# Nested Strassen products for theta and phi, and an earlier data sum in the last image, in an attention and non-local kernel

## The chip, the cores and the metric

The kernel runs on one core of a Trainium2 chip. The metric is the device time of one execution in microseconds. Times within an execution come from the trace of one profiled execution, counted from the start of its span.

## The reference, cut to what matters

The batch is 8 images of 512 channels and 32 x 32 = 1024 positions, all in float32. Everything on TensorE is a 1x1 convolution, which is a matrix product over the channels, or an attention product.

```python
def conv(x, W, b): return einsum('bchw,oc->bohw', x, W) + b
# layer 0: attention with 8 heads of 64 channels
q, k, v = conv(x, Wq, bq), conv(x, Wk, bk), conv(x, Wv, bv)
o = softmax(q^T k / 8) v                      # per image and head
x = x + conv(o, Wp, bp)
# layer 1: non-local block with 256 inner channels, n = 1024
g, theta, phi = conv(x, g_w, g_b), conv(x, theta_w, theta_b), conv(x, phi_w, phi_b)
f = einsum('bcn,bdn->bcd', theta, phi) / n
y = einsum('bcd,bdn->bcn', f, g)
z = conv(y, W_w, W_b) + x
out = (z - mean) * rsqrt(var + 1e-5) * gamma + beta   # mean and var over all images, per channel
```

## The kernel before, in words

**Work of one image.** The loop `for b in range(B)` in the main part goes over the images. For each it does attention (scores `ps`, line 578, and weighted values `po`, line 604), then q, v and k of the *next* image, then the projection `project` (the product of Wp with o, PSUM tiles `pp`), then theta and phi together (`theta_phi`, PSUM tiles `ptp`, result `tp`), then `nonlocal_` (g in `pg`, f in `pf`, `pwf`, and z in `pz`). The last image, number 7, has its own branch: the non-local work of image 6 is done inside it, and the normalization of o comes after that.

**Products.** A convolution is one round of the Strassen-Winograd scheme: the weights are cut in 2 x 2 blocks, the data in 2 x 2 quarters named 11, 12, 21, 22, and seven products replace eight. The table `SEVEN` gives for each product its name, the weight block (0 to 6), the data it takes, its PSUM slot and the parts of the result it is read into. Blocks 3 to 6 are sums of weights; t1 to t4 are sums of data, made by `more_sums` (line 252): t1 = 12 - 11, t2 = 22 - t1, t3 = 22 - 12, t4 = 21 - t2. `seven` (line 342 issues the matmuls) goes through such a table; `between` maps a product's number to work that is emitted after it. `EARLY` and `LATER` are other orders of the seven; the last image's projection uses `LATER`: 11, s1t1, 12, s2t2 and so on. When a product is done, VectorE reads its PSUM slot: `first` (line 766 for theta and phi, with the bias added; line 737 for the projection) or an addition (line 772, line 448).

**Nesting.** For the projection of images 1 to 6 two of the seven products are themselves cut into seven inner products. The table is then `FIVE`, and `nested` (line 299 issues it) yields one inner product at a time; `STEPS` says after which of the 40 matmuls of `FIVE` an inner step is emitted. Inner sums of data come from `inner_parts` (line 264), inner sums of weights lie beside their block in the weight tile (`extra`). Each inner step's PSUM part is read by VectorE at once; two slots alternate, so a step waits until the step two before it has been read. The products of v use inner products whose output has positions on the partitions (`pv_in`, line 418, tiles of 128 columns).

**Theta and phi.** `theta_phi` computes both in one product with positions on the partitions: the plain `SEVEN`, eight matmuls of 128 x 128 by 256 columns each, each matmul two records in the profile.

**Weights.** The weights of one convolution are loaded in units (`UNITS`) into a pool of four buffers of 1792 columns, `wr`, in the order of a plan. Block 0 of some is loaded by itself as "first". `load_w` (its DMA is line 163) issues the next unit on the queue of SyncE (SP). `kept` holds copies in DRAM, with the sums. Theta and phi have two units of 768 KB, blocks (3, 4, 2) and (6, 5, 1). SP issues its DMAs in program order, and a DMA waits for the one eight before it.

**The last image.** After g of image 6, `normalize` multiplies o by the reciprocals of the softmax denominators, in four VectorE operations (line 684) that wait for the tile r (DMAs of line 679); then come t1 and t2 of o. On SP's queue stand, in this order: r (4 DMAs), the first unit of theta and phi, `put_away` (4 writes of g and wf of image 6, lines 906 and 907), `reload` of the z of images 0 to 3 (16 DMAs of 512 KB, line 918), the bias `tpb` (line 752), the second unit of theta and phi, the weights of g, four chunks of z of image 5 (line 925).

```python
            for one in normalize(nxt["d"]):
                one()
            load_w()
            put_away(b - 1)
            for i, tag in enumerate("vqk"):
                reload(i, mats, tag)
            reload(3, foldp, "fold")
        tpb = load_tpb(b)
```

**Image 0.** Its weights are made from the raw ones: sums of blocks on VectorE, then copies to DRAM with `keep`. Its product is plain.

Of the kernel before, what the change touches and what calls it, by code (L numbers as in the profile page):

```python
# [11 lines left out]
ALU = mybir.AluOpType  # L12
# [4 lines left out]
P = 128  # L17
# [13 lines left out]
def unshifted(ctx: ExitStack, tc: tile.TileContext, a: dict, out: bass.AP):  # L31
    nc = tc.nc
# [29 lines left out]
    def pe(ins):  # L62
        tc.keep_in_program_order(ins)
# [47 lines left out]
    for b in range(1, B):  # L111
# [2 lines left out]
    loaded, ahead = [], {"unit": [], "first": []}  # L114

    PAIRS = ((1, 6), (3, 4), (5, 2))
    UNITS = {"WqT": PAIRS, "WkT": PAIRS, "WvT": PAIRS, "WpT": ((1, 2), (3, 4, 5), (6,)), "tp": ((3, 4, 2), (6, 5, 1)),
             "WgT": (range(7),)}
    WIDTH = 14 * P
    INNER = (1, 2)  # L120

    class Weights:

# [4 lines left out]
        def __getitem__(self, at):  # L128
            if not isinstance(at, tuple):
                return self.at[at]  # L130
            return self.at[at[1]][(slice(None), *at[2:])]

        def place(self, n, t):
            size, to = 2 * self.half, 0
            blocks = (0,) if n == "first" else UNITS[self.name][n]
            for i in blocks:
                self.at[i] = t[:, to:to + size].rearrange("p (k f) -> p k f", k=2)
                to += size
                if n != "first" and len(blocks) == 2:
                    self.extra[i] = t[:, to:to + 3 * P].rearrange("p (i f) -> p i f", i=3)  # L140
                    to += 3 * P
            self.tiles[n] = t[:, :to]
            return blocks

        def whole(self, n):
            t = self.tiles[n]
            if n == "first" or len(UNITS[self.name][n]) != 2:
                return t
            return t.rearrange("p (b f) -> p b f", b=2)[:, :, :2 * self.half]

# [52 lines left out]
    def inner_weights(w, i):  # L203

        a11, a12, a22, a21, s2, s3, s4 = w.inner(i)
        return [lambda to=to, l=l, r=r, op=op: dve(nc.vector.tensor_tensor(to, l, r, op))
                for to, l, r, op in ((s3, a11, a21, ALU.subtract), (a21, a21, a22, ALU.add), (s2, a21, a11, ALU.subtract),
                                     (s4, a12, s2, ALU.subtract))]

    def keep_inner(w):  # L210

# [72 lines left out]

    STEPS = [0] * 4 + [1] * 14

    def nested(name, w, data, tags, first, add):

        slots = [bank(tag, f"{name}_in_{tag}") for tag in tags]
        goes_to = {1: ("11", "21", False), 2: ("21", "t4", True)}
        for n, (q, di, begins) in enumerate(goes_to[i] for i in INNER):
            a, d = w.inner(INNER[n]), data[f"inner {di}"]
            pair = slots[::-1] if n % 2 else slots
            begun = set()
            for _, wi, di, s, reads in SEVEN:
                ps = pair[s % 2 if s < 2 else 1][:, s // 2, n % 2 * 256:(n % 2 + 1) * 256]
                pe(nc.tensor.matmul(ps, a[wi], d[di], start=s not in begun, stop=True, skip_group_check=True))  # L299
                begun.add(s)  # L300
                for to, is_first in reads:
                    c = rows(q).start + int(to[0]) - 1
                    at = cols(q).start + (int(to[1]) - 1) * 256
                    (first if is_first and begins else add)((slice(c, c + 1), slice(at, at + 256)), ps)
                yield

    def seven(name, w, data, positions_out, first, add, between=None, early=False,
              by_chunk=False, inner=False):

        nk, half = w.shape[2], w.shape[3]
        tags = list(free)
        free[:] = [tags[3], tags[1], tags[0], tags[2]] if early else [tags[3], tags[1], tags[2], tags[0]]
        slots, begun = {}, set()
        steps, counts = iter(()), iter(STEPS if inner else ())
        if inner:
            free[:] = [tags[1], tags[2], tags[3], tags[0]]
            steps = nested(name, w, data, tags[2:], first, add)

        def read(reads, ps):
            for to, is_first in reads:
                (first if is_first else add)(to, ps)

        products = FIVE if inner else LATER if early == "later" else EARLY if early else SEVEN
        for n, (what, wi, di, s, reads) in enumerate(products):
            if s not in slots or early and what == "t4":
                slots[s] = bank(tags[s], f"{name}_{s}_{n}")
                begun -= {one for one in begun if one[0] == s}
            ps, d = slots[s], data[di]  # L330
            if positions_out:
                parts = [(ps.rearrange("p h (i f) -> p (h i) f", f=half)[:, i, :], i * half // 512,
                          lambda k, i=i: d[:, k, i * P:(i + 1) * P], lambda k: w[:, wi, k, :])
                         for i in range(512 // P)]
            else:
                parts = [(ps[:, m, :], m, lambda k, m=m: w[:, wi, k, m * P:(m + 1) * P], lambda k: d[:, k, :])
                         for m in range(half // P)]
            work = [(*part, k) for part in parts for k in range(nk)]
            if by_chunk and what in ("11", "s1t1"):
                work.sort(key=lambda one: one[4])  # L340
            for i, (to_ps, at, lhsT, rhs, k) in enumerate(work):
                pe(nc.tensor.matmul(to_ps, lhsT(k), rhs(k), start=(s, at) not in begun, stop=(k == nk - 1),  # L342
                                    skip_group_check=True))
                begun.add((s, at))
                for _ in range(next(counts, 0)):
                    next(steps)
            read(reads, ps)
            if between and n in between:
                between[n]()
# [377 lines left out]
            return o["o"], lambda ps: denominators(1, ps), lambda d: normalize((first_den, d))  # L727
        return o["o"], all_denominators, normalize

    def project(b, xt, o, w, between, data=None):  # L730
        def first(q, ps):
            if isinstance(q[0], slice):
                ps = ps.unsqueeze(1)
# [4 lines left out]
                if b == B - 1 and q in ("11", "22"):  # L738
                    dve(ins)

        if not data:
            data = data_sums(quarters_of(o), f"o_{b}", (1, 2), pin=dve)
            between = {**between, 1: lambda: more_sums(data, (3, 4), dve)}
        seven(f"pp_{b}", w, data, False, first, add_to(xt), between, early=b == B - 1 and "later", inner=0 < b < B - 1)


    tps = []
# [7 lines left out]
    def theta_phi(b, w, data, tpb, between):  # L755
        tp = mats.tile([P, NB, 2 * CI], F32, tag="o", name=f"tp_{b}")
        tps[:] = [tp]

        def at(q):
            return tp[:, (int(q[1]) - 1) * NB // 2:int(q[1]) * NB // 2, (int(q[0]) - 1) * CI:int(q[0]) * CI]  # L760

        def as_tp(ps):
            return ps.rearrange("p h (i f) -> p (h i) f", f=CI)

        def first(q, ps):
            ins = nc.vector.tensor_tensor(at(q), as_tp(ps), tpb[:, int(q[0]) - 1].to_broadcast([P, NB // 2, CI]),
                                          ALU.add)
            if q == "11":
                dve(ins)

        seven(f"ptp_{b}", w, data, True, first,
              lambda q, ps: nc.vector.tensor_tensor(at(q), at(q), as_tp(ps), ALU.add),  # L772
              {0: lambda: "t3" in data or more_sums(data, (3, 4), pin=dve), **between})
        return tp

    def f_sums(b, tp, k0):
# [233 lines left out]
    for b in range(B):  # L1010
        last = b == B - 1
        nxt = {}
        if not last:
            nxt["x"] = load_x(b + 1)

# [58 lines left out]
        else:  # L1074
# [1 line left out]
                      {4: lambda: nxt.update(d=denominators(next_bank(f"den_{b}_1")[:, 0, :]))})  # L1076
            z[b - 1] = [held["x"][:, cc, :] for cc in range(CC)]
            between = {4: late_unit(b - 1, 0, sums_now=False)}
            for one in normalize(nxt["d"]):
                one()  # L1080
            load_w()
            put_away(b - 1)
            for i, tag in enumerate("vqk"):
                reload(i, mats, tag)
            reload(3, foldp, "fold")
        tpb = load_tpb(b)
        w = weights("WpT", sums_done=True)
        project(b, xt, o, w, between, nxt.get("o"))
        if b == 0:
            w_p = w  # L1090
        load_w("first")
# [8 lines left out]
            z[b] = [xt[:, cc, :] for cc in range(CC)]  # L1100
        of_theta = []
        w = weights("tp")
        between = {} if last else {5: lambda: b < B - 2 and of_theta.append(f_sums(b, tps[0], 0))}
        if b == 0:
            weight_sums(w, corner["tp"], (3, 4, 5), dve)

            def nest_p(i):
                for one in inner_weights(w_p, i):
                    one()

            between.update({1: lambda: weight_sums(w, corner["tp"], (6,), dve), 2: lambda: nest_p(1), 3: lambda: nest_p(2)})
        tp = theta_phi(b, w, data, tpb, between)
        if b == 0:
            keep("tp", w)
            kept["WpT"] = dict(kept["plain"])
            keep("WpT", w_p, (0,))
            load_w()
        load_w("first")
        load_w(times=2)

        def before_wf():
            if last:
# [243 lines left out]
```

## Time and profile before

| what | value |
|---|---|
| time, median of 3 runs (lowest, highest) | 2118.22 us (2117.09, 2118.61) |
| time of the profiled execution | 2118.56 us |
| its span | 2116.7 us |
| granted TensorE clock, mean over the span | 0.994 |
| TensorE busy | 2090.3 us, 99% of the span |
| VectorE busy | 1403.2 us, 66% |
| ScalarE busy | 790.3 us, 37% |
| GpSimd busy | 525.9 us, 25% |
| moved by DMA | 243.56 MB, 115 GB/s in the mean |

The profiled execution's time is its span and 1.9 us around it; it lies 0.34 us above the median. The page gives averages over the whole span. What a change in one stage is worth has to be read from the timeline, the waits and the chain of work inside that stage.

### The profile page before, as it was taken

The page shows a single profiled execution, that of the slowest core. Times are in us where ns is not written, and L with a number is a line of the kernel's source. Part 1 is how long each engine was busy: PE and PEld are TensorE (multiplying, and loading weights), DVE is VectorE, ACT ScalarE, POOL GpSimd, SP SyncE. Part 2 cuts the span into 40 slices and gives each one's busy share as a digit, 9 for nine tenths or more (in the row PEclk, how much of TensorE's full clock was granted, in tenths as well). Part 3 has the DMA queues.
Part 4 walks back from the last instruction along what each step waited for, and adds up shares of the span by engine and source line. Part 5 has one row for each costly group of instructions (what it writes and reads, how often), then busy time and mean ns, then how long its engine had stood idle before and what let it go on. Part 6 is the DMA issues. An engine that isn't in the chain of part 4 may idle for free.

```text
span 2116.7 us, 33247 instructions
## 1 busy us (share of the span) xinstructions
PE 2090.3 (99%) x13486; PEld 1172.5 (55%) x13486; DVE 1403.2 (66%) x2051; ACT 790.3 (37%) x1045; POOL 525.9 (25%) x392
## 2 busy tenths in 40 slices
PE   9999999999999999999999999999999999999996
PEld 4535863357733677337763377633875348733362
DVE  5587567765578655786557766677565775567636
ACT  1464204642046410564106631166303653066016
POOL 0012900138001370014601155011640119011000
PEclk9999999999999999999999999999999999999998
DMA  6253533244232532425314253133544235222758
GB/s 229 83 148 76 174 147 111 40 92 141 100 117 40 120 110 98 120 40 141 122 62 125 40 152 121 72 101 41 170 139 140 39 63 169 75 31 40 268 188 319
DMA packets 71728, 243.56 MB, mean 115 GB/s; under 512 B 12688, under 2 KB 21136, under 8 KB 69520
## 3 DMA queue, kind: packets, MB, share of 16 engines
q1 hardware_dynamic: 60640, 215.01, 30.4%
q0 software_dynamic: 9072, 24.78, 9.5%
q8 instruction: 108, 1.77, 0.3%
q10 hardware_dynamic: 1856, 1.56, 0.3%
q14 instruction: 52, 0.43, 0.1%
HBM read 160.45 MB, written 47.32 MB: 98 GB/s over the span
## 4 chain that ended last, share of the span: by engine, by line
PE 97%; DVE 1%; ACT 1%; DMA 1%; issue 0%; SPq 0%; DVEq 0%
PE ps L578 21%; PE po L604 21%; PE ptp L342 9%; PE pp L342 7%; PE pv_in L418 6%; PE pq_in L421 6%; PE pk_in L421 6%; PE pg L342 4%; PE pz L342 3%; PE pf L801 2%; PE pp_in_s L299 2%; PE pq L388 1%; PE pq L342 1%; PE pv L385 1%; PE pv L342 1%; PE pk L388 1%
## 5 line engine op out<-in xcount | busy, mean ns | idle before, releaser
L581 ACT ACTIVATE e<-ps 128x1024 f32<-128x1024 f32 x512 | 523.0, 1025 | 422.9 <-PE ps L578 412.2
L587 DVE TENSOR_TENSOR acc<-acc,e 128x1024 f32<-128x1024 f32 x384 | 469.9, 1224 | 103.1 <-ACT e L581 92.9
L578 PE MATMUL ps<-q,k 64*64 64x512 f32 x4096 | 529.3, 589 | 0.0
L604 PE MATMUL po<-e,v 64*64 64x512 f32 x4096 | 528.6, 589 | 0.0
L617 POOL DMA_DIRECT2D fold<-acc x189 | 144.8, 766 | 1358.3 <-PE ps L578 690.6
L604 PEld LDWEIGHTS po<-e,v 64*64 64x64 f32 x4096 | 156.6, 133 | 282.9 <-issue 275.5
L578 PEld LDWEIGHTS ps<-q,k 64*64 64x64 f32 x4096 | 155.5, 133 | 283.5 <-issue 277.3
L844 ACT ACTIVATE g<-pg,gb 128x512 f32<-128x512 f32 x31 | 21.3, 688 | 447.0 <-PE pg L342 446.9
L585 DVE TENSOR_TENSOR acc<-e,e 128x1024 f32<-128x1024 f32 x64 | 78.3, 1224 | 121.2 <-ACT e L581 119.0
L342 PE MATMUL ptp<-w_tp,t_x 128*128 128x256 f32 x512 | 114.4, 379 | 0.0
L342 PE MATMUL pp<-t_o,w_WpT 128*128 128x512 f32 x208 | 103.4, 605 | 4.6 <-DVE t_o L252 4.6
L342 PEld LDWEIGHTS ptp<-w_tp,t_x 128*128 128x128 f32 x512 | 97.3, 190 | 13.2
L342 PE MATMUL ptp<-w_tp,x 128*128 128x256 f32 x384 | 86.8, 379 | 0.0
L342 PEld LDWEIGHTS ptp<-w_tp,x 128*128 128x128 f32 x384 | 73.0, 190 | 13.3 <-issue 3.8
L429 DVE TENSOR_TENSOR v<-v,pv_in 128x256 f32<-128x256 f32 x112 | 46.3, 421 | 43.8 <-PE pv_in L418 37.3
L429 DVE TENSOR_TENSOR k<-k,pk_in 128x256 f32<-128x256 f32 x112 | 46.8, 421 | 39.4 <-PE pk_in L421 35.0
L342 PE MATMUL pp<-o,w_WpT 128*128 128x512 f32 x144 | 67.7, 592 | 0.0
L427 ACT COPY v<-pv_in 128x256 f32<-128x256 f32 x84 | 31.4, 374 | 95.8 <-DVE T_pv L429 25.5
L427 ACT COPY k<-pk_in 128x256 f32<-128x256 f32 x84 | 31.3, 373 | 91.6 <-PE pk_in L421 89.9
L684 POOL TENSOR_TENSOR o<-o,r 128x1024 f32<-128x1024 f32 x28 | 65.3, 2372 | 0.0
L772 DVE TENSOR_TENSOR tp<-tp,ptp 128x1024 f32<-128x1024 f32 x24 | 29.3, 1221 | 51.2 <-PE ptp L342 51.2
L737 DVE SCALAR_TENSOR_TENSOR x<-pp,bp,x 128x512 f32<-128x512 f32 x52 | 37.6, 746 | 38.5 <-PE pp L342 38.5
(230 smaller groups left out, 2954.8 us busy)
## 6 DMA issues: line engine op xcount, KB each, us to landing
fold<-acc POOLq DMA_DIRECT2D x189, 128.0 KB, 3.1
w_WqT<-kept_WqT SPq DMA_DIRECT2D x21, 896.0 KB, 4.9
w_WvT<-kept_WvT SPq DMA_DIRECT2D x21, 896.0 KB, 5.0
w_WkT<-kept_WkT SPq DMA_DIRECT2D x21, 896.0 KB, 6.2
r<-den_d SPq DMA_DIRECT2D x32, 512.0 KB, 6.8
x<-in_x_dram SPq DMA_DIRECT2D x30, 512.0 KB, 5.9
spill<-x SPq DMA_DIRECT2D x24, 512.0 KB, 4.0
z<-spill SPq DMA_DIRECT2D x24, 512.0 KB, 9.9
```

What stands on the lines that cost most here:

```text
L342: pe(nc.tensor.matmul(to_ps, lhsT(k), rhs(k), start=(s, at) not in begun, stop=(k == nk - 1), skip_group_check=True))
L418: pe(nc.tensor.matmul(ps[:, i, :], d[:, i * P:(i + 1) * P], a, start=start and not i, stop=True, skip_group_check=True))
L421: pe(nc.tensor.matmul(ps, a, d, start=start, stop=True, skip_group_check=True))
L427: nc.scalar.copy(piece(q, i, j), ps)
L429: dve(nc.vector.tensor_tensor(piece(q, i, j), piece(q, i, j), ps, ALU.add))
L578: pe(nc.tensor.matmul(ps[c * P // 2:(c + 1) * P // 2, j, :], k[r, p, keys], q[r, p, h * 512:(h + 1) * 512], start=True, stop=True, skip_gr ...
L581: nc.scalar.activation(e, ps, AF.Exp, scale=SCALE)
L585: nc.vector.tensor_tensor(accs[u], es[u, 0], e, ALU.add)
L587: ins = nc.vector.tensor_tensor(accs[u], accs[u], e, ALU.add)
L604: pe(nc.tensor.matmul(ps[j * D:(j + 1) * D, r, :], v[keys, m, (2 * p + j) * D:(2 * p + j + 1) * D], e[keys, j, :], start=(m == 0), stop=(m ...
L617: nc.gpsimd.dma_start(to, part_of, accum_op=ALU.add)
L684: dve((engine or nc.vector).tensor_tensor(at, at, of, ALU.mult))
```

## The change

It has three parts. First, theta and phi of images 1 to 7 use `FIVE` with two nested products instead of `SEVEN`: the product of block 2 with t4 and that of block 1 with the quarter 21 are each done as seven inner products, one inner step after each of the wide matmuls 25 to 38. t4 and the inner sums of t4 and 21 are made on GpSimd; t3 is made after the read of s1t1. For this the weights of theta and phi get three units, blocks (1, 2) with their inner sums, (3, 4, 5) and (6); their inner sums are made on VectorE at the start of image 1. The loads are issued at other places: units 1 and 2 and g's weights after the projection, three units of q after theta and phi. In image 0 g's weights are loaded only after theta and phi.

Second, in the last image t1 of o is made after two of the four products of `normalize`, and t2 after the other two. Third, the last image's `tpb` is loaded ahead of `put_away` and `reload`.

```diff
-    UNITS = {..., "WpT": ((1, 2), (3, 4, 5), (6,)), "tp": ((3, 4, 2), (6, 5, 1)),
+    UNITS = {..., "WpT": ((1, 2), (3, 4, 5), (6,)), "tp": ((1, 2), (3, 4, 5), (6,)),
...
-    STEPS = [0] * 4 + [1] * 14
-    def nested(name, w, data, tags, first, add):
+    INNER = {"p": (FIVE, ((1, "21", "11", False), (2, "t4", "21", True)), [0] * 4 + [1] * 14),
+             "tp": (FIVE, ((2, "t4", "21", True), (1, "21", "11", False)), [0] * 24 + [1] * 14)}
+    def nested(name, w, data, tags, first, add, goes_to, positions_out):
...
+                if positions_out:
+                    ps = ps.rearrange("p (i f) -> p i f", f=P)
+                    for i in range(2):
+                        pe(nc.tensor.matmul(ps[:, i, :], d[di][:, i * P:(i + 1) * P], a[wi], start=start and not i,
+                                            stop=True, skip_group_check=True))
...
 def theta_phi(b, w, data, tpb, between):
+        def sums():
+            if "t3" not in data:
+                for i in (4,) if b else (3, 4):
+                    more_sums(data, (i,), dve, nc.gpsimd if b else None)
+            if b:
+                for of in ("t4", "21"):
+                    inner_sums(data, of, dve, nc.gpsimd)
+        def third_sum():
+            if "t3" not in data:
+                more_sums(data, (3,), dve)
-              {0: lambda: "t3" in data or more_sums(data, (3, 4), pin=dve), **between})
+        seven(f"ptp_{b}", w, data, True, first, add, {0: sums, **({1: third_sum} if b else {}), **between}, inner="tp" if b else None)
...
     for b in range(B):
+        if b == 1:
+            nest(w_tp, 1)
+            nest(w_tp, 2)
+            keep("tp", w_tp, (0,))
+            load_w()
...
-            for one in normalize(nxt["d"]):
+            nxt["o"] = data_sums(quarters_of(o), f"o_{b}", ())
+            for n, one in enumerate(normalize(nxt["d"])):
                 one()
+                if n % 2:
+                    more_sums(nxt["o"], (n // 2 + 1,), dve)
+            between[1] = lambda: more_sums(nxt["o"], (3, 4), dve)
             load_w()
+            tpb = load_tpb(b)
             put_away(b - 1)
             for i, tag in enumerate("vqk"):
                 reload(i, mats, tag)
             reload(3, foldp, "fold")
-        tpb = load_tpb(b)
+        if not last:
+            tpb = load_tpb(b)
...
-        between = {} if last else {5: lambda: b < B - 2 and of_theta.append(f_sums(b, tps[0], 0))}
+        between = {} if last else {4 if b else 5: lambda: b < B - 2 and of_theta.append(f_sums(b, tps[0], 0))}
...
         tp = theta_phi(b, w, data, tpb, between)
         if b == 0:
-            keep("tp", w)
             kept["WpT"] = dict(kept["plain"])
             keep("WpT", w_p, (0,))
             load_w()
+            keep("tp", w, ("first", 1, 2))
+            w_tp = w
         load_w("first")
-        load_w(times=2)
+        load_w(times=3 if b else 2)
```

More of the change, by code (lines that the diff above doesn't have):

```diff
@@ L116, in unshifted @@
     PAIRS = ((1, 6), (3, 4), (5, 2))
-    UNITS = {"WqT": PAIRS, "WkT": PAIRS, "WvT": PAIRS, "WpT": ((1, 2), (3, 4, 5), (6,)), "tp": ((3, 4, 2), (6, 5, 1)),
+    UNITS = {"WqT": PAIRS, "WkT": PAIRS, "WvT": PAIRS, "WpT": ((1, 2), (3, 4, 5), (6,)), "tp": ((1, 2), (3, 4, 5), (6,)),
              "WgT": (range(7),)}
     WIDTH = 14 * P
-    INNER = (1, 2)
     class Weights:
@@ L131, in __getitem__, with blocks, roomy @@
             return self.at[at[1]][(slice(None), *at[2:])]
+        def blocks(self, n):
+            return (0,) if n == "first" else UNITS[self.name][n]
+        def roomy(self, n):
+            return len(self.blocks(n)) == 2
         def place(self, n, t):
             size, to = 2 * self.half, 0
-            blocks = (0,) if n == "first" else UNITS[self.name][n]
+            blocks = self.blocks(n)
             for i in blocks:
@@ L138, in place @@
                 to += size
-                if n != "first" and len(blocks) == 2:
+                if self.roomy(n):
                     self.extra[i] = t[:, to:to + 3 * P].rearrange("p (i f) -> p i f", i=3)
@@ L146, in whole @@
             t = self.tiles[n]
-            if n == "first" or len(UNITS[self.name][n]) != 2:
+            if not self.roomy(n):
                 return t
@@ L208, in inner_weights, with nest @@
                                      (s4, a12, s2, ALU.subtract))]
+    def nest(w, i):
+        for one in inner_weights(w, i):
+            one()
     def keep_inner(w):
@@ L282, in unshifted @@
     FIVE = (SEVEN[0], SEVEN[1], SEVEN[2], SEVEN[3], ("s3t3", 5, "t3", 0, (("22", False), ("21", False))))
-    STEPS = [0] * 4 + [1] * 14
-    def nested(name, w, data, tags, first, add):
+    INNER = {"p": (FIVE, ((1, "21", "11", False), (2, "t4", "21", True)), [0] * 4 + [1] * 14),
+             "tp": (FIVE, ((2, "t4", "21", True), (1, "21", "11", False)), [0] * 24 + [1] * 14)}
+    def nested(name, w, data, tags, first, add, goes_to, positions_out):
         slots = [bank(tag, f"{name}_in_{tag}") for tag in tags]
-        goes_to = {1: ("11", "21", False), 2: ("21", "t4", True)}
-        for n, (q, di, begins) in enumerate(goes_to[i] for i in INNER):
-            a, d = w.inner(INNER[n]), data[f"inner {di}"]
+        for n, (outer, of, q, begins) in enumerate(goes_to):
+            a, d = w.inner(outer), data[f"inner {of}"]
             pair = slots[::-1] if n % 2 else slots
@@ L298, in nested @@
                 ps = pair[s % 2 if s < 2 else 1][:, s // 2, n % 2 * 256:(n % 2 + 1) * 256]
-                pe(nc.tensor.matmul(ps, a[wi], d[di], start=s not in begun, stop=True, skip_group_check=True))
+                start = s not in begun
                 begun.add(s)
-                for to, is_first in reads:
-                    c = rows(q).start + int(to[0]) - 1
-                    at = cols(q).start + (int(to[1]) - 1) * 256
-                    (first if is_first and begins else add)((slice(c, c + 1), slice(at, at + 256)), ps)
+                if positions_out:
[3 more added lines that the diff above has]
+                                            stop=True, skip_group_check=True))
+                else:
+                    pe(nc.tensor.matmul(ps, a[wi], d[di], start=start, stop=True, skip_group_check=True))
+                for to, is_first in reads:
+                    i, j = int(to[0]) - 1, int(to[1]) - 1
+                    if positions_out:
+                        to = q, i, j
+                    else:
+                        c, at = rows(q).start + i, cols(q).start + j * 256
+                        to = slice(c, c + 1), slice(at, at + 256)
+                    (first if is_first and begins else add)(to, ps)
                 yield
     def seven(name, w, data, positions_out, first, add, between=None, early=False,
-              by_chunk=False, inner=False):
+              by_chunk=False, inner=None):
         nk, half = w.shape[2], w.shape[3]
@@ L315, in seven @@
         slots, begun = {}, set()
-        steps, counts = iter(()), iter(STEPS if inner else ())
+        steps, counts = iter(()), iter(())
         if inner:
             free[:] = [tags[1], tags[2], tags[3], tags[0]]
-            steps = nested(name, w, data, tags[2:], first, add)
+            products, goes_to, counts = INNER[inner]
+            counts = iter(counts)
+            steps = nested(name, w, data, tags[2:], first, add, goes_to, positions_out)
+        else:
+            products = LATER if early == "later" else EARLY if early else SEVEN
         def read(reads, ps):
@@ L323, in read @@
                 (first if is_first else add)(to, ps)
-        products = FIVE if inner else LATER if early == "later" else EARLY if early else SEVEN
         for n, (what, wi, di, s, reads) in enumerate(products):
@@ L728, in attention, with project @@
         return o["o"], all_denominators, normalize
-    def project(b, xt, o, w, between, data=None):
+    def project(b, xt, w, between, data):
         def first(q, ps):
@@ L739, in first @@
                     dve(ins)
[L741 to L744, printed above, removed]
+        seven(f"pp_{b}", w, data, False, first, add_to(xt), between, early=b == B - 1 and "later",
+              inner="p" if 0 < b < B - 1 else None)
     tps = []
@@ L759, in at, with as_tp, add @@
         def at(q):
+            if isinstance(q, tuple):
+                q, i, j = q
+                m, c = (int(q[1]) - 1) * NB // 2 + j * NB // 4, (int(q[0]) - 1) * CI + i * P
+                return tp[:, m:m + NB // 4, c:c + P]
             return tp[:, (int(q[1]) - 1) * NB // 2:int(q[1]) * NB // 2, (int(q[0]) - 1) * CI:int(q[0]) * CI]
-        def as_tp(ps):
-            return ps.rearrange("p h (i f) -> p (h i) f", f=CI)
+        def as_tp(q, ps):
+            return ps if isinstance(q, tuple) else ps.rearrange("p h (i f) -> p (h i) f", f=CI)
         def first(q, ps):
-            ins = nc.vector.tensor_tensor(at(q), as_tp(ps), tpb[:, int(q[0]) - 1].to_broadcast([P, NB // 2, CI]),
-                                          ALU.add)
-            if q == "11":
-                dve(ins)
-        seven(f"ptp_{b}", w, data, True, first,
-              lambda q, ps: nc.vector.tensor_tensor(at(q), at(q), as_tp(ps), ALU.add),
-              {0: lambda: "t3" in data or more_sums(data, (3, 4), pin=dve), **between})
+            to, of = at(q), tpb[:, int((q[0] if isinstance(q, tuple) else q)[0]) - 1]
+            if isinstance(q, tuple):
+                of = of[:, :, q[1] * P:(q[1] + 1) * P]
+            ins = nc.vector.tensor_tensor(to, as_tp(q, ps), of.to_broadcast(list(to.shape)), ALU.add)
+            if q == "11" or b:
+                dve(ins)
+        def add(q, ps):
+            ins = nc.vector.tensor_tensor(at(q), at(q), as_tp(q, ps), ALU.add)
+            if b:
+                dve(ins)
+        def sums():
+            if "t3" not in data:
+                for i in (4,) if b else (3, 4):
+                    more_sums(data, (i,), dve, nc.gpsimd if b else None)
+            if b:
+                for of in ("t4", "21"):
[4 more added lines that the diff above has]
+        seven(f"ptp_{b}", w, data, True, first, add, {0: sums, **({1: third_sum} if b else {}), **between}, inner="tp" if b else None)
         return tp
@@ L1085, in unshifted @@
             reload(3, foldp, "fold")
-        tpb = load_tpb(b)
+        if not last:
+            tpb = load_tpb(b)
         w = weights("WpT", sums_done=True)
-        project(b, xt, o, w, between, nxt.get("o"))
+        project(b, xt, w, between, nxt["o"])
         if b == 0:
@@ L1102, in unshifted @@
         w = weights("tp")
-        between = {} if last else {5: lambda: b < B - 2 and of_theta.append(f_sums(b, tps[0], 0))}
+        between = {} if last else {4 if b else 5: lambda: b < B - 2 and of_theta.append(f_sums(b, tps[0], 0))}
         if b == 0:
             weight_sums(w, corner["tp"], (3, 4, 5), dve)
[L1107 to L1111, printed above, removed]
+            between.update({1: lambda: weight_sums(w, corner["tp"], (6,), dve), 2: lambda: nest(w_p, 1),
+                            3: lambda: nest(w_p, 2)})
         tp = theta_phi(b, w, data, tpb, between)
         if b == 0:
-            keep("tp", w)
             kept["WpT"] = dict(kept["plain"])
```

## The prediction

> **What bounds the kernel now.** I read the page's busy times, then what TensorE (PE) waited for.
>
> ```profile
> PE 2090.3 (99%) x13486; PEld 1172.5 (55%) x13486; DVE 1403.2 (66%) x2051; ACT 790.3 (37%) x1045; POOL 525.9 (25%) x392
> ```
>
> ```profile
> PE count L1152 <- DVE good L1150: 8.5, 1, 8.5
> PE pp L342 <- DVE t_o L252: 4.6, 1, 4.6
> PE warm_ps L471 <- DVE folds L486: 1.1, 1, 1.1
> PE den L644 <- ACT got L238: 0.3, 1, 0.3
> ```
>
> PE is the bound; the one sizable wait inside the images is 4.6 us in the last, for t1 of o. Fewer PE cycles shorten the kernel, unless a new wait takes their place. The chain of work gives the price of theta and phi in image 2, and of a 128-column matmul in v:
>
> ```profile
> 797.00 24.17 PE ptp L342 x112
> ...
> ```
>
> ```profile
> 734.93 17.09 PE pv_in L418 x153
> ```
>
> A record of `ptp` (256 columns) costs 24.17/112 = 0.2158 us, one of 128 columns 17.09/153 = 0.1117 us. Then the last image, by stretches of time (columns: window, PE, PEld, DVE, ACT, POOL busy, granted clock, DMA share, GB/s), and SP's queue in its timeline:
>
> ```profile
> 1984.00:1986.00 2.00, 0.00 (x0) 0.00 (x0) 1.08 (x1) 0.00 (x0) 0.00 (x0) 1.00 0.97 368
> 1986.00:1988.00 2.00, 0.00 (x0) 0.00 (x0) 2.00 (x3) 0.00 (x0) 0.00 (x0) 0.57 1.06 424
> 1988.00:1990.00 2.00, 1.53 (x2) 0.83 (x3) 1.97 (x3) 0.00 (x0) 0.00 (x0) 0.50 1.03 375
> 1990.00:1995.00 5.00, 5.00 (x9) 2.05 (x8) 1.50 (x3) 0.00 (x0) 0.00 (x0) 0.69 1.02 404
> 1995.00:2000.00 5.00, 5.00 (x13) 2.22 (x12) 4.30 (x5) 0.00 (x0) 0.00 (x0) 1.00 1.03 415
> ```
>
> ```profile
> 1970.01 8.76 SPq L679 DMA_DIRECT2D r<-den_d  x4
> 1978.81 0.59 SPq L163 DMA_DIRECT2D w_tp<-kept_tp  x1
> ...
> 1981.49 19.85 SPq L918 DMA_DIRECT2D z<-spill  x16
> 2002.35 0.33 SPq L752 DMA_DIRECT2D tpb<-in_theta_b_dram  x1
> 2003.58 0.33 SPq L752 DMA_DIRECT2D tpb<-in_phi_b_dram  x1
> 2004.91 0.33 SPq L163 DMA_DIRECT2D w_tp<-kept_tp  x1
> ```
>
> The reader is to see two things: the idle PE comes back at half clock, and the DMA engines are full from 1984 on, with the second unit of theta and phi behind 16 reloads of z.
>
> **What the Trainium skill says.** "TensorE: Matmul & The Clock Gate", section "What's actually happening": after an idle window of about 3.4 us the array runs at half rate, until it has been busy for about as long; the window runs freely. The trace agrees: after 4.59 us of idling the eight matmul records of s1t1, 3.60 us elsewhere, took 5.99, and the next group began 5.82 instead of 3.43 us on: 2.39 us lost. "DMA: Bandwidth & Descriptors", section "Where 436 GB/s comes from", puts a ceiling of 435 GB/s; the trace moved 404 to 415 here. "VectorE: DVE Perf Modes", section on the TRN2 errata, gives a float32 tensor_tensor as (N + 151)/0.96 ns: 424 at N = 256, 1224 at 1024; the trace has 421 and 1221.
>
> **Part 1, theta and phi nested.** Removed per image: two products of 16 records, 2 x 16 x 0.2158 = 6.906 us. Added: 2 x 7 inner products of 2 matmuls, 56 records at 0.1117 = 6.255 us. Saved: 0.652 us an image, for seven images **-4.56 us**. All of it lies on PE, so on the path.
>
> DVE (VectorE): seven reads of 1.22 us become six of 1.22 and 14 of 0.42, 13.2 against 8.5 us, beside PE's 23.5. Inner steps come after matmuls 25 to 38, each with its wide matmul (0.4316) and 4 x 0.1117: a period of 0.878 us, two periods for a slot to be read. From the start of `ptp`: s4 starts at 10.36, its wide matmuls end near 17.1, the eighth step's read ends at 17.9, then s4's read to 19.05, then the ninth step's to 19.4. The eleventh step needs that: due at 19.57, its weight load 0.24 earlier. Late by 0 to 0.3 us; I take 0.05 an image, **+0.35** in all. The others have 0.7 us of slack.
>
> GpSimd (POOL): t2 is done 3.7 us into `ptp`; t4 there takes 2.37 (line 684's row), four inner sums of t4 0.73 each (line 264's row): done at 9.0, needed at 10.8. The sums of 21 end at 11.9, needed near 17. POOL has nothing else in that window; if this cover went, 1.8 us late would begin to cost. The theta sums of DVE (2.6 us) move after the last product; s3t3's two reads then end 2.5 us after `ptp`, all sums about 5 us later, before pf, which starts 8.6 us after `ptp`. Nothing there is late in images 1 to 5.
>
> The loads of images 1 to 6: unit 1 waits for the same buffer as before, issued 4.5 us ahead of `ptp` (792.3 for 796.84) and needed 3.45 us into it; this load takes 4.2 us in the median: covered. The eight inner sums of weights at image 1's start (2.4 us of DVE) and one copy to DRAM are covered by the ring of twelve blocks and an SP queue that is not awaited there.
>
> Two places lose. **Image 0**: g's weights now arrive near 301 us, and their four sums stand on DVE behind the last read of `tp` (304.87 to 306.09). The second sum is what s1t1 of g needs: 306.00 + 0.34 + 0.42 = 306.8, PE wants 306.04. **+0.8**. **Image 6**: pf follows two steps of scores, 1.72 us after `ptp`. One read of 1.22 us ended before; two end 2.5 us after: **+0.8**.
>
> **Part 2, t1 between the products.** Products 0 and 1 end at 1979.96 in the trace (they wait for the first r only), t1 then at 1981.1, before PE ends product 11 at 1983.88. The 4.59 us of idling and the 2.39 us of slow clock go: 6.98 us. Products 2 and 3 end at 1987.3 as now (r lands at 1984.8), 12 is due at 1987.5, s2t2 with t2 (1988.5) at 1991. So `ptp` of image 7 would start at 2011.46 - 6.98 = 2004.48.
>
> **What is late next.** s1t1 of theta and phi takes block 3. Before, blocks 3 and 4 were in the first unit, loaded ahead of the reloads; after, they are in the second, and its `load_w` still stands behind `reload`. The queue is bound by bytes: after r's landing at 1984.8 come unit 0 (0.92 MB), tpb (0.26), g and wf (1.57), z (16 x 0.524 = 8.39), unit 1 (0.79), 11.93 MB; at 408 GB/s 29.2 us, so it lands at **2014.1**. The same sum for before (11.80 MB) gives 2013.8; its trace has issue 2004.91 plus 9.0 to landing, 2013.9. PE ends product 11 at 2007.93 and waits 6.2 us. s1t1 starts at 2014.2; before it was 2014.91. **-0.7**. And 6.2 us of idling halves the clock again: the measured **+2.4**, bounds 0 (no whole idle window) and 3.4.
>
> **Part 3, tpb early.** Bytes moved forward by 0.26 MB, 0.6 us for the z; none for unit 1. It waits for finished things. Zero.
>
> **Sum.** -4.56 + 0.35 + 0.8 + 0.8 - 0.7 + 2.4 = -0.9 us. Against the profiled execution's 2118.56 that is 2117.65; that execution is 0.34 above the median, so **2117.3**.
>
> **Rivals.**
> - *The clock stays up in the wait*: without the 2.4, 2114.9. For it: the window runs freely. Against: 4.59 us sufficed before. Chance 0.12.
> - *The second unit is in time*, so that all of the 6.98 us is kept: 2117.3 - 1.7 - 6.98 = 2108.6. It would need 8.4 MB less ahead of it. Chance 0.04.
> - *Slower: DVE holds the inner steps.* If the ninth step's read comes a whole read of s4 later than I reckon, the eleventh waits 1.05 us (1.14 less the margin), seven times, 7.35 instead of 0.35: 2124.3. From 0.18 us a step on, (0.9 + 0.35)/7, the kernel is slower than before. For it: the margin is only about 0.1 us. Against: DVE is less than 60% busy there. Chance 0.14.
> - *My case*: 0.70.
>
> **The numbers.** My own case spans the bounds of the clock (-2.4, +1.0), of the steps (-0.35, +1.7) and about 0.7 for the landing: 2114.9 to 2120.8. Reaching to the others, the range is 2114.6 to 2121.6. About 0.2% (4.2 us) is what a measurement can tell from no change: faster than 2114.0 is the second rival and the edge of the first, 0.10; slower than 2122.5 most of the third and an edge of mine, 0.13; between, 0.77.
>
> **What would show it.** Right: `ptp` of images 1 to 6 takes 23.5 us; idle PE near 306 and before image 6's pf; no wait for t_o; a PE wait of about 6 us for a w_tp DMA in image 7, then records at half clock. Wrong: PE waits for DVE reads inside `ptp`, or no wait for w_tp.

## The result, and the profile after

| | median | lowest to highest | runs |
|---|---|---|---|
| before | 2117.61 us | 2116.63 to 2119.01 | 12 |
| after | 2117.44 us | 2115.86 to 2118.17 | 12 |

The ratio is 0.9997, with a 95% interval of 0.9988 to 1.0006: no difference that these runs can tell. The forecast was 2117.3 us. It rested on a change of -0.9 us; the medians differ by -0.17 us, and the interval allows anything from -2.5 to +1.3. The profiled execution took 2116.34 us with a span of 2114.6, so it lies 1.1 us below its own median, where that of before lies 0.95 us above the median of these twelve runs: the two spans differ by 2.1 us, far more than the medians, and part of that is a difference between executions.

The busy times of the page after, and the waits of PE (columns: us in total, times, longest):

```profile
PE 2085.1 (99%) x13654; PEld 1173.4 (55%) x13654; DVE 1428.3 (68%) x2144; ACT 789.9 (37%) x1045; POOL 584.9 (28%) x454
```

```profile
PE count L1204 <- DVE good L1202: 8.6, 1, 8.6
PE ptp L365 <- DMA w_tp<-kept_tp: 6.3, 1, 6.3
PE warm_ps L494 <- DVE folds L509: 1.1, 1, 1.1
PE pg L365 <- DVE w_WgT L107: 0.7, 1, 0.7
PE pf L860 <- DVE tp L800: 0.7, 1, 0.7
PE den L667 <- ACT got L247: 0.3, 1, 0.3
```

The wait of 4.6 us for t_o is gone, and three new ones stand there: 6.3 us for the weights of theta and phi, and two of 0.7 us. PE is busy for 5.2 us less: 4.2 of that are the nested products, about 0.8 lie in the kernel's first records, and about 0.3 in records at half clock (all three are worked out below). The work went down, and waiting took the place of most of it.

The chain of work in image 2 shows the nested products at the price that was worked out:

```profile
796.49 10.79 PE ptp L365 x50
807.28 0.45 PE ptp_in_s L313 x4
807.72 0.43 PE ptp L365 x2
...
816.06 0.50 PE ptp_in_s L313 x4
...
819.19 0.87 PE ptp L365 x4
820.06 8.58 PE pg L365 x20
```

From the first line to g's is 820.06 - 796.49 = 23.57 us, against 24.17 before: 0.60 us saved. One inner step of the 14 takes 0.50 instead of 0.44: that is the eleventh, which waits 0.06 us for VectorE.

The last image, in the timeline of PE and of SP's queue (start, us, engine, line, operation, count; in brackets the idle time before and what ended it). First PE before the change:

```profile
1980.28 3.60 PE L342 MATMUL pp<-o,w_WpT 128*128 128x512 f32 x8
1988.47 5.99 PE L342 MATMUL pp<-t_o,w_WpT 128*128 128x512 f32 x8 [4.59 <-DVE t_o L252]
...
2011.46 3.62 PE L342 MATMUL ptp<-w_tp,x 128*128 128x256 f32 x16
2014.91 7.07 PE L342 MATMUL ptp<-w_tp,t_x 128*128 128x256 f32 x32
```

Then PE and SP's queue after it:

```profile
1977.30 3.60 PE L365 MATMUL pp<-o,w_WpT 128*128 128x512 f32 x8
1980.74 3.60 PE L365 MATMUL pp<-t_o,w_WpT 128*128 128x512 f32 x8
...
2001.34 3.62 PE L365 MATMUL ptp<-w_tp,x 128*128 128x256 f32 x16
2011.23 9.20 PE L365 MATMUL ptp<-w_tp,t_x 128*128 128x256 f32 x32 [6.28 <-DMA w_tp<-kept_tp]
2020.27 0.59 PE L365 MATMUL ptp<-w_tp,x 128*128 128x256 f32 x2
```

```profile
1976.14 0.34 SPq L774 DMA_DIRECT2D tpb<-in_theta_b_dram  x1
...
1981.26 18.05 SPq L961 DMA_DIRECT2D z<-spill  x16
2000.32 1.60 SPq L168 DMA_DIRECT2D w_tp<-kept_tp  x2
```

s1t1 of the projection follows product 11 at once, at 1980.74. But theta and phi stop after their own product 11, until unit 1 has landed behind the sixteen reloads. Its two products s1t1 and s2t2 then take 2020.27 - 2011.23 = 9.04 us, where 2 x 3.453 = 6.91 is their time at full clock: 2.13 us lost. The granted clock was at half when PE went on and still was at 2014 (columns as in the prediction's stretches of time: the third number from the end is the clock, the last one GB/s):

```profile
2012.00:2014.00 2.00, 2.00 (x7) 1.56 (x6) 0.00 (x0) 0.00 (x0) 0.34 (x1) 0.50 1.00 403
```

The chain shows what PE waited for:

```profile
1974.76 6.49 DMA r<-den_d
...
1981.26 7.91 DMA z<-spill
...
1989.19 11.07 DMA z<-spill
...
2000.32 10.78 DMA w_tp<-kept_tp
...
2011.23 9.63 PE ptp L365 x34
```

For 30 us, from r's landing to unit 1's, the path that sets the end is one chain of DMAs. Before, over the same stretch, it was PE from 1988.47 on:

```profile
1978.17 6.65 DMA r<-den_d
1984.92 2.36 DVE o L684 x2
...
1988.47 23.15 PE pp L342 x48
```

### The profile page after: what moved, and what is told of

Same layout as the page of the kernel before. It is cut to its first block, busy times and chain, and to the rows that moved or that the text cites. A ratio compares the mean times of both kernels' runs of the same rounds, so it can differ in the third digit from the quotient of the medians.

```text
span 2114.6 us, 33849 instructions
## 1 busy us (share of the span) xinstructions
PE 2085.1 (99%) x13654; PEld 1173.4 (55%) x13654; DVE 1428.3 (68%) x2144; ACT 789.9 (37%) x1045; POOL 584.9 (28%) x454
## 4 chain that ended last, share of the span: by engine, by line
PE 95%; DMA 2%; DVE 1%; ACT 1%; issue 0%; SPq 0%; DVEq 0%
PE po L627 21%; PE ps L601 21%; PE ptp L365 7%; PE pv_in L441 6%; PE pq_in L444 6%; PE pk_in L444 6%; PE pp L365 6%; PE pg L365 4%; PE pz L365 3%; PE ptp_in_s L313 2%; PE pf L844 2%; PE pp_in_s L316 2%; PE pq L411 1%; PE pv L365 1%; PE pv L408 1%; PE pq L365 1%
## 5 line engine op out<-in xcount | busy, mean ns | idle before, releaser
L604 ACT ACTIVATE e<-ps 128x1024 f32<-128x1024 f32 x512 | 522.6, 1024 | 422.5 <-PE ps L601 411.8
L365 PE MATMUL ptp<-w_tp,t_x 128*128 128x256 f32 x400 | 98.2, 386 | 6.3 <-DMA w_tp<-kept_tp 6.3
L365 PEld LDWEIGHTS ptp<-w_tp,t_x 128*128 128x128 f32 x400 | 73.7, 194 | 15.0 <-issue 6.7
L365 PE MATMUL ptp<-w_tp,x 128*128 128x256 f32 x272 | 69.6, 380 | 0.0
L441 PE MATMUL pv_in<-w_WvT,i_t_x 128*128 128x128 f32 x448 | 59.2, 275 | 0.0
L444 PE MATMUL pk_in<-i_t_x,w_WkT 128*128 128x256 f32 x224 | 57.8, 381 | 0.0
```

What stands on the lines that cost most here:

```text
L441: pe(nc.tensor.matmul(ps[:, i, :], d[:, i * P:(i + 1) * P], a, start=start and not i, stop=True, skip_group_check=True))
L444: pe(nc.tensor.matmul(ps, a, d, start=start, stop=True, skip_group_check=True))
L604: nc.scalar.activation(e, ps, AF.Exp, scale=SCALE)
```

## The experiments

The theory under test: each part gains by itself, and together the gain of the last image turns into a wait for a load, because the new split of the weights has put blocks 3 and 4 behind the reloads. The rivals: the nesting gains nothing; the last image is bound by its bytes whatever the order; the slow records after the wait come from something else than idling. The experiments were measured in two groups, each with its own runs of before: the median of before was 2117.52 us for "Part 2 alone" and "All waits removed", and 2117.62 us for the other four. Ratios are to these.

**Part 1 alone.** The whole change, with the last image's normalization and bias load as they were:

```diff
-            for n, one in enumerate(normalize(nxt["d"])):
+            for one in normalize(nxt["d"]):
                 one()
-                if n % 2:
-                    more_sums(nxt["o"], (n // 2 + 1,), dve)
+            more_sums(nxt["o"], (1, 2), dve)
...
-            tpb = load_tpb(b)
             put_away(b - 1)
...
-        if not last:
-            tpb = load_tpb(b)
+        tpb = load_tpb(b)
```

> Part 1 alone: theta and phi nested, the last image's normalization and bias load as before. My theory: each part gains by itself, and they lose together. Here PE still waits about 4.6 us for t1 of o, and because theta and phi of image 7 start late, their unit 1 has landed (2014.1 against 2014.9 in the frame of before), so no wait for it. Seven nestings at 0.60 us less 0.9 (image 0) and 0.7 (image 6) give -2.6 us, about 2115.0 against 2117.6 for before. Rival, that the nesting gains nothing and the last image is not the cause: 2117.4 as the whole change.

Measured: 2115.36 us, ratio 0.9988 (0.9982 to 0.9995), 2.3 us below before, where 2.6 were expected. Its waits of PE:

```profile
PE pp L365 <- DVE t_o L261: 4.0, 1, 4.0
...
PE pg L365 <- DVE w_WgT L107: 0.7, 1, 0.7
PE pf L860 <- DVE tp L800: 0.7, 1, 0.7
PE ptp L365 <- DVE t_x L261: 0.3, 1, 0.3
```

The wait for t_o is back, and none for the weights is left; where PE starts theta and phi later, unit 1 is there. A short wait for a data sum of x, in the last image, was not foreseen. So the nesting does gain, and part 1 alone is faster than the whole change, by 2.1 us of the medians.

**Parts 2 and 3 alone.** The kernel before, with t1 between the products and the early bias:

```diff
+            nxt["o"] = data_sums(quarters_of(o), f"o_{b}", ())
-            for one in normalize(nxt["d"]):
+            for n, one in enumerate(normalize(nxt["d"])):
                 one()
+                if n % 2:
+                    more_sums(nxt["o"], (n // 2 + 1,), dve)
+            between[1] = lambda: more_sums(nxt["o"], (3, 4), dve)
             load_w()
+            tpb = load_tpb(b)
             put_away(b - 1)
...
-        tpb = load_tpb(b)
+        if not last:
+            tpb = load_tpb(b)
```

> Parts 2 and 3 alone, on the kernel before, with plain products for theta and phi. My theory: blocks 3 and 4 are in the first unit there, loaded ahead of the reloads, so the 4.6 us of waiting and the 2.4 us at half clock are kept as a gain: -7.0 us, about 2110.6. The second unit lands at about 2013.8 and block 6 is due at 2014.8, so no new wait. Rival, that the reloads of z bound the last image whatever PE does: about 2117.

Measured: 2111.17 us, ratio 0.9966 (0.9954 to 0.9978), 6.5 us below before, where 7.0 were expected. All its waits of PE but the one at the kernel's end:

```profile
PE warm_ps L471 <- DVE folds L486: 1.1, 1, 1.1
PE den L644 <- ACT got L238: 0.3, 1, 0.3
```

With the old units PE does not wait in the last image at all. The rival of a last image bound by its bytes falls: the bytes are the same, only the block that is needed second stands in front of them.

**Part 2 alone.** The same without the early bias: `tpb` is loaded behind the reloads, as before.

```diff
-            tpb = load_tpb(b)
             put_away(b - 1)
...
-        if not last:
-            tpb = load_tpb(b)
+        tpb = load_tpb(b)
```

> Part 2 alone on the kernel before, with the bias of theta and phi still loaded behind the reloads. My theory: it lands near 2012 in the frame of before, product 11 of image 7 can't be read earlier, and s2t2, which needs its slot at 2011.4, waits until that read is done at about 2013.2: 1.9 us of the gain of 7.0 are lost, about 2112.5. Rival, that part 3 is worth nothing: 2110.6 as with it.

Measured: 2113.39 us, ratio 0.9982 (0.9976 to 0.9989); 2.2 us above the kernel with the early bias. In its waits:

```profile
PE ptp L342 <- DVE tp L766: 1.6, 1, 1.6
...
PE pp L342 <- DVE o L684: 0.7, 1, 0.7
```

The first line is the forecast wait of s2t2 for the read of product 11. With it the first three products of theta and phi take 12.19 us, against 10.36 with the early bias: 1.83 us lost, where 1.9 were expected. The second, for the second half of the normalized o, was not expected; in the kernel with the early bias it is absent. In this execution VectorE could use the last r only 6.5 us after the start of `pp`; in the other seven profiles it was 3.7 to 4.6 us after it. Why is open, and since this execution lies 1.3 us above its median, most of the others probably had no such wait. So part 3 is worth about 1.8 us where theta and phi can go on. In the changed kernel it is probably worth nothing, since PE waits for the weights there anyway; that was not tried.

**The reloads behind the weights.** The whole change with its sixteen reloads moved:

```diff
-            for i, tag in enumerate("vqk"):
-                reload(i, mats, tag)
-            reload(3, foldp, "fold")
...
         load_w(times=3 if b else 2)
+        if last:
+            for i, tag in enumerate("vqk"):
+                reload(i, mats, tag)
+            reload(3, foldp, "fold")
```

> The whole change, with the sixteen reloads of z moved behind the loads of units 1 and 2 of theta and phi and of g's weights. My theory: the 6.3 us of waiting and the 2.4 us at half clock both go, -8.7 us, about 2108.7. Rival, that the queue is bound by bytes anyway and another load becomes late (z, ww or the g and wf of an earlier image): the wait moves and the time stays between 2112 and 2117.

Measured: 2108.81 us, ratio 0.9956 (0.9943 to 0.9970), 8.6 us below the changed kernel. Its timeline:

```profile
2002.24 3.62 PE L365 MATMUL ptp<-w_tp,x 128*128 128x256 f32 x16
2005.70 7.07 PE L365 MATMUL ptp<-w_tp,t_x 128*128 128x256 f32 x32
2012.60 0.59 PE L365 MATMUL ptp<-w_tp,x 128*128 128x256 f32 x2
```

```profile
1995.57 3.75 SPq L168 DMA_DIRECT2D w_tp<-kept_tp  x2
2002.44 0.32 SPq L168 DMA_DIRECT2D w_WgT<-kept_WgT  x1
2002.81 16.29 SPq L961 DMA_DIRECT2D z<-spill  x16
```

Wait and slow records are both gone, and nothing else became late. The queue even stood still before 1995.57, since a weight buffer has to be free first, and the last reload was issued at 2019.1, where the changed kernel issued it by 1999.3: PE did not need them sooner. The gain of 8.6 us is the wait and the half clock (6.28 + 2.13 = 8.4) to within the noise, so the order of the queue was the cause of this loss.

**The wait filled.** To part the wait from the clock, seven matmuls of 512 columns stand between the products 11 and s1t1 of theta and phi in image 7:

```diff
+            if name == f"ptp_{B - 1}" and what == "s1t1":
+                for i in range(7):
+                    pe(nc.tensor.matmul(ps[:, 0, :], data["11"][:, 0, :P], data["11"][:, 0, :], start=True, stop=True,
+                                        skip_group_check=True))
```

> The whole change, with seven matmuls of 512 columns (about 6.0 us) put between the products 11 and s1t1 of theta and phi in image 7; they write into the slot of s1t1, which that product overwrites, so they change no result. They stand in the wait for unit 1 and keep PE busy. My theory: the wait itself costs what it did, but the clock stays up, so the 2.4 us go: about 2115.0. If the slow records after the wait came from something else than idling, for instance the full DMA engines: 2117.4, with the records still slow.

Measured: 2115.38 us, ratio 0.9989 (0.9982 to 0.9996), 2.1 us below the changed kernel.

```profile
2005.67 6.17 PE L363 MATMUL ptp<-x 128*128 128x512 f32 x14
2012.39 7.14 PE L369 MATMUL ptp<-w_tp,t_x 128*128 128x256 f32 x32 [0.55 <-DMA w_tp<-kept_tp]
```

s1t1 starts no earlier than in the changed kernel (10.17 us after product 11's start, there 9.89), 0.55 us after the last of the added matmuls. Both products then take 2019.37 - 2012.39 = 6.98 us, full clock, and the DMA engines are as full as in the changed kernel:

```profile
2012.00:2014.00 2.00, 1.61 (x8) 1.46 (x9) 0.00 (x0) 0.00 (x0) 1.25 (x2) 1.00 0.98 401
```

In this stretch the granted clock is 1.00 where the changed kernel had 0.50, at 401 GB/s where that had 403. So the slow records came from the idling, not from the transfers. Adding useless work made the kernel faster by what the clock had cost.

**All waits removed.** The kernel with the reloads behind the weights, and two edits against the waits of 0.7 us: g's weight sums of image 0 on GpSimd, and s3t3 read into 21 first.

```diff
-    def weights(name, sums_done=False, pin=lambda ins: None):
+    def weights(name, sums_done=False, pin=lambda ins: None, engine=None):
...
-                weight_sums(w, corner[name], pin=pin)
+                weight_sums(w, corner[name], pin=pin, engine=engine)
...
-             "tp": (FIVE, (
+             "tp": ((*FIVE[:4], ("s3t3", 5, "t3", 0, (("21", False), ("22", False)))), (
...
-                      weights("WgT"), before_wf,
+                      weights("WgT", engine=None if b else nc.gpsimd), before_wf,
```

> As the kernel with the reloads behind the weights, and besides: the four sums of g's weights in image 0 on GpSimd, and s3t3 of theta and phi read into 21 before 22, so that the first half of pf's inputs is ready one read earlier. My theory: the 0.7 us at g's s1t1 of image 0 and the 0.7 us at pf of image 6 go, -1.4 us: about 2107.3 where the other gives 2108.7. Rival, that these two waits only move to the next instruction: no difference.

Measured: 2106.28 us, ratio 0.9947 (0.9934 to 0.9961), 2.5 us below the kernel with the reloads moved alone, where 1.4 were expected. The spans of the two profiled executions differ by 1.7 us (2107.0 and 2105.3), of which the traces show 0.93 in image 0 and 0.66 in image 6; the other 0.8 us of the medians, which come from the two groups, are not explained. All its waits of PE:

```profile
PE count L1205 <- DVE good L1203: 8.6, 1, 8.6
PE warm_ps L494 <- DVE folds L509: 1.1, 1, 1.1
PE den L667 <- ACT got L247: 0.3, 1, 0.3
```

Both waits are gone, and the rival that they only move falls. This version is faster than both kernels, by 0.53% against before.

## Why the prediction was right, step by step

The range held, and nearly every term of the sum is found in the trace. That the median came within 0.2 us of the forecast is also luck: a change of -0.9 us cannot be told from none in these runs, and the median of before itself was 2118.22 us in its first three runs and 2117.61 in twelve. In the trace:

| step | predicted | measured in the profiled execution |
|---|---|---|
| nesting, seven images, with the wait of the eleventh step | -4.56 + 0.35 | 7 x (23.57 - 24.17) = -4.2 |
| image 0, g's weight sums | +0.8 | +0.93: theta and phi's end to pf 9.52 us, before 8.59 |
| image 6, pf | +0.8 | +0.73: `ptp` to pf 26.27 us, before 26.14, less the 0.60 saved |
| image 7, start of s1t1, from the start of `pp` | -0.7 | 33.93 us, before 34.63: -0.70 |
| image 7, half clock | +2.4 | +2.13 |
| sum | -0.9 | -1.1 |

- **The landing of unit 1** was the step that decided. Summing the bytes behind r gave 29.2 us from r's landing; the trace has 1981.24 to 2011.10, 29.9 us. A forecast from the removed wait alone would have been 8.7 us lower, the 2108.6 us of the second rival, and the kernel with the reloads moved measured 2108.81.
- **The start of s1t1** came out at -0.70 us by two errors that cancel. Counted from the moment VectorE could use the last r, s1t1 started 29.99 us later before (2014.91 - 1984.92) and 29.96 after (2011.23 - 1981.27): nothing was gained there. But r landed 4.6 us after the start of `pp` before and 4.0 after, a difference that the prediction did not have and that lies within the spread of the profiles; unit 1 landed 0.7 us later behind it than reckoned. The same spread decides whether product 12 waits for the second half of o. By the timeline it was due at 1980.28 + 2 x 3.43 = 1987.14 in the frame of before, and not at 1987.5 as the prediction has it; with that half ready at 1987.3 there was no margin. Here r came early, and in the kernel of part 2 alone it came late and PE waited 0.7 us.
- **The half clock** was costed as in before. It was 2.39 us there, 2.13 in the changed kernel and 1.80 in part 1 alone (5.23 us from s1t1 to the next product, less 3.43). The Trainium skill ("TensorE: Matmul & The Clock Gate", "What's actually happening") has a freely running window, which would make the loss vary so; the runs show that it varies, not why.
- **Image 0** was a little more than reckoned: 0.69 us is the wait proper, the rest is the first weight load after it, which no longer lies beside other work.
- **The slower rival**, VectorE holding the inner steps, did not come: 0.06 us a step, near the lower end. Before most reads of inner steps VectorE was idle for 0.45 us.
- **GpSimd** was done in time, but with less margin than the 1.8 us of the prediction: in image 2 the sums of t4 ended at 806.5, and the first inner step starts at 807.3. The lost 1 us is one inner sum that took 1.71 us instead of 0.73, the fourth of t4, and it is the same one in each of images 1 to 6. It runs beside t3, which the change has VectorE make just then, and t3 itself takes 1.31 us there instead of 1.22. In image 7, where t3 is made earlier, all eight sums take 0.72 us, and sums that run beside VectorE's reads of PSUM are not longer. That the two operations hold each other up is what this suggests; no run moved t3 to show it.
- **What the sum does not hold** is the rest of the span's 2.1 us: 0.84 us lie in the first 30 us, before anything that was changed. The first group of 16 matmul records took 7.18 us in the profile after and 8.02 before, where the weight loads of the first three stand up to 0.86 us apart instead of 0.43, as they do at half clock in image 7; the granted clock reads 1.00 there in both profiles, so that this is the clock is argued and not shown. In six other profiles of this study the group took 7.7 to 8.3 us. It differs from execution to execution, and is one reason why the median moved by 0.2 and not by 2 us.

## What to carry to other kernels

When a change makes an engine reach a stage earlier, list what that stage loads and where those loads stand in their queue: on a full queue a load lands when the bytes ahead of it have passed; here the last one landed 29 to 30 us after r in both kernels, though only in the changed one was PE ready for it by then. Splitting or regrouping a load changes which block comes first; here 0.8 MB on the wrong side of 8.4 MB cost 8.6 us. And cost an idle stretch of TensorE twice, once as waiting and once as the slow clock after it.

## What the runs showed of the hardware

- Idle TensorE came back at half rate after waits of 4.0, 4.6 and 6.3 us, and lost 1.8 to 2.4 us each time, on top of the wait. In the profiled executions the granted clock stayed at 1.00 after waits of 0.7 and 1.6 us in the kernel of part 2 alone. Five of its 21 executions, though, have a mean granted clock of 0.995 or 0.994 and took 2115.05 to 2116.98 us, while the others have 0.996 and at most 2114.70; there is no trace of them. Filling 6.2 of the 6.7 us before unit 1 with matmuls kept the full rate.
- With the DMA engines full, the last load of theta and phi's weights landed 29.1 us after r as the last of 11.80 MB (before), and 29.9 us after it as the last of 11.93 MB (after): 405 and 399 GB/s.
- A GpSimd subtraction of 128 x 256 float32 took 0.72 to 0.73 us seven times of eight in theta and phi of images 1 to 6, and 1.71 the eighth time, beside VectorE's t3, which is a subtraction of 128 x 1024 with both inputs in SBUF (the on-chip memory, as opposed to PSUM).
